# Two adds on VectorE in place of two identity products on TensorE, in the attention loop of a graph network

## The chip, the cores and the metric

The kernel runs on one core of one Trainium2 chip. The metric is the device time of one execution in microseconds (us), the median of several runs. The profile is of one execution; times in it are counted from the start of its span.

## The reference, cut to what matters

Two graph layers run over 3327 nodes with 512 features. Both use the same sparse adjacency matrix: about eight neighbours a node, itself included. Each layer ends with a residual and a normalisation.

```python
# layer 0, per head h (4 heads of 128 features)
feats  = einsum('nf,hfo->hno', X, W)
logits = leaky_relu(e_s[:, :, None] + e_n[:, None, :], 0.2)     # e_s, e_n: feats times a vector
attn   = softmax(logits where A, axis=-1)
out    = relu(einsum('hnm,hmo->hno', attn, feats) + b)
x      = layernorm(x + out)
# layer 1: a gated sum of an attention over the neighbours and of their plain sum
x      = layernorm(x + sigmoid(attn_a * x_a + attn_b * x_b))
```

The change concerns the line of `out`: the sum over a node's neighbours of attention weight times feature row, plus the bias `b`, before the relu.

## The kernel before, in words

**First part (to about 210 us).** The kernel finds every node's neighbours in the adjacency matrix, sorts the nodes by degree, and writes the features of all nodes to a table in device memory. The nodes are then worked on in 26 tiles of 128. Since they are sorted, all nodes of tile `j` fit into `CAPS[j]` neighbours besides the node itself: 4 to 14. Nodes with more are in tiles 0 and 12 (`T0`), the first of the two groups of 12 and 14 tiles, which carry one more gathered "stair" row.

**Layer 0 (about 216 to 560 us).** The loop at L878 goes through the tiles in `order0`: tiles 11 and 10, then 0 to 9, then the second group with long and short tiles in turn. Each engine takes its instructions in the order in which the loop issues them; nothing reorders them. Step `i` of the loop does the following.

- `gather` (L667, L661) for the tile of step `i + 3`: POOL issues an indirect DMA for each neighbour slot, which brings one feature row for each of the 128 nodes. For the second group the first two slots come in one DMA (L661): the node's input row and its own feature row. The rows land in buffers of up to six slots, of which there are seven (`GB`); a tile takes one to three. A gather into a used buffer waits until its last reader is done.
- `publish`: the normalised rows of earlier tiles are written to the table of layer 1 (ScalarE L847, VectorE L850 and L851, then a DMA: from SP for the first group, a scatter from POOL, L145, for the second).
- `columns2` of step `i - 2`: ScalarE copies transposed rows (L836), TensorE multiplies them by eight columns (L839).
- `attend` of step `i`: the weighted sum. TensorE first puts the bias into the accumulator by a product of the identity with it (L804). Then, slot by slot, the gathered row is multiplied in place by its four weights, one for each head: by VectorE in one instruction (L812), or for each third slot by ScalarE in four (L810). TensorE adds each row to the accumulator by a product with the identity (L815). The accumulator is in PSUM, and there are two.
- VectorE reads the accumulator of step `i - 1`, applies the relu and adds the input row (L893). For the second group that input row lies in the tile's first gather buffer. The statistics (L712, L713) follow, and after every few tiles the inverse square root (L721 to L728). TensorE transposes the result (L832), and VectorE copies the columns of step `i - 2` (L843).
- In steps 1 to 7 the lists of the second group are sorted with TensorE (L548); in step 7 VectorE copies the sorted lists (L553, L554). In step 8 it spreads the stair of the second group (`climb`, L599 and L600).
- `weigh_a` and `weigh_b` of step `i + 1`: the softmax weights from the gathered rows of that tile (VectorE L769 to L795, ScalarE's exponential L782). They need all of the tile's gathers to have landed.

**Layer 1 (from about 560 us)** gathers from the second table and has its own loop (L1072). In it VectorE also sums rows in pairs in place (L1022).

Of the kernel before, what the change touches and what calls it, by code (L numbers as in the profile page):

```python
# [25 lines left out]
CAPS = (14, 12, 11, 10, 9, 9, 8, 8, 7, 6, 6, 5) + (14, 13, 11, 10, 10, 9, 9, 8, 8, 7, 7, 6, 5, 4)  # L26
# [53 lines left out]
def sparse_pass(  # L80
# [39 lines left out]
    nc = tc.nc  # L120
    N, F = out.shape
# [8 lines left out]
    T0 = (0, NG[0])  # L130
# [27 lines left out]
    ident = const.tile([P, P], F32, name="ident")  # L158
    ones = const.tile([P, P], F32, name="ones")
    bias0 = const.tile([P, F], F32, name="bias0")  # L160
# [22 lines left out]
    def row1(j):  # L183
        g, i = place(j)
        return x1[g][:, i, :]
# [162 lines left out]
    for b, n in enumerate(STAIRS):  # L348
        o = sum(STAIRS[:b])
# [244 lines left out]
    def climb(g, pool, psum):  # L594

        of = pool.tile([P, B + H], F32, tag="of", name=f"of{g}")
        nc.vector.tensor_copy(of[:, :B], srt[g][:, 0, C0 + 1 : S + 1])
        nc.vector.tensor_copy(of[:, B:], srt[g][:, 0, S + 2 : S + 2 + H].bitcast(F32))
        nc.tensor.matmul(psum, to_row, of, start=True, stop=True)  # L599
        nc.vector.tensor_mul(of[:, :B], psum[:, :B], step_of)  # L600
        id_ = pool.tile([P, 1], F32, tag="id_", name=f"id_{g}")
        nc.vector.tensor_reduce(id_, of[:, :B], AX.X, ALU.add)
        nc.vector.tensor_copy(ids2[g], id_)
        nc.vector.tensor_copy(es2[g], psum[:, B:])
# [39 lines left out]
    def gather(table, j):  # L644


        g, i = place(j)
        ahead = 0 if table is table1 else 1 + g
        c = CAPS[j] + ahead
        more = j in T0  # L650
        n = (c + more + U - 1) // U
        w = (c + more + n - 1) // n
        got = []
        for q0 in range(0, c + more, w):
            m = min(w, c - q0)
            buf = gp.tile([P, U, ROW], F32, tag="g", name=f"g_{nc.next_id()}", bufs=GB)
            for q in range(q0, q0 + m):
                s = q - ahead + 1
                if ahead == 2 and q < 2:
                    if q == 0:  # L660
                        nc.gpsimd.indirect_dma_start(  # L661
                            out=buf[:, 0:2, :].rearrange("p t w -> p (t w)"), out_offset=None,
                            in_=own1.rearrange("n t w -> n (t w)"),
                            in_offset=bass.IndirectOffsetOnAxis(ap=srt[g][:, i, S + 1 : S + 2], axis=0),
                        )
                    continue
                nc.gpsimd.indirect_dma_start(  # L667
                    out=buf[:, q - q0, :], out_offset=None, in_=table[:, :],
                    in_offset=bass.IndirectOffsetOnAxis(ap=srt[g][:, i, s : s + 1], axis=0),
                )  # L670
            o = 1 if ahead == 2 and q0 == 0 else 0
            if m > o:
                got.append((q0 + o - ahead + 1, m - o, buf, o))
        if more:
            stair[j] = buf[:, m, :]
            nc.gpsimd.indirect_dma_start(
                out=stair[j], out_offset=None, in_=table[:, :],
                in_offset=bass.IndirectOffsetOnAxis(ap=ids2[g][:, 0:1], axis=0),
            )
        return got  # L680
# [73 lines left out]
    order0 = first[-2:][::-1] + first[:-2] + second[-3:-2]  # L754
# [42 lines left out]
            small = psx.tile([P, B * H], F32, tag="pcol", name=f"to_rows{j}", bufs=2)  # L797
            ws2[j] = to_rows(m0, small, f"n{j}", w[:, C0 + 1 :, :])

    def attend(j):  # L800

        w = ws[j]
        acc = accs[j] = ps.tile([P, F], F32, tag="acc", name=f"acc{j}", bufs=2)
        nc.tensor.matmul(acc, ident, bias0, start=True, stop=False)  # L804
        for s0, n, buf, o in got[j]:
            for s in range(s0, s0 + n):
                gv = buf[:, o + s - s0, 0:F].rearrange("p (h o) -> p h o", h=H)
                if s % 3 == 2:
                    for h in range(H):
                        nc.scalar.activation(gv[:, h, :], gv[:, h, :], AF.Copy, scale=w[:, s, h : h + 1])  # L810
                else:
                    nc.vector.tensor_tensor(  # L812
                        gv, gv, w[:, s, :].rearrange("p (h o) -> p h o", o=1).to_broadcast([P, H, FO]), ALU.mult
                    )
                nc.tensor.matmul(  # L815
                    acc, ident, buf[:, o + s - s0, 0:F], start=False, stop=(s == CAPS[j] and j not in T0)
                )
        if j in T0:
            gv = stair[j][:, 0:F].rearrange("p (h o) -> p h o", h=H)
            nc.vector.tensor_tensor(  # L820
                gv, gv, ws2[j].rearrange("p (h o) -> p h o", o=1).to_broadcast([P, H, FO]), ALU.mult
            )
            nc.tensor.matmul(acc, to_node, stair[j][:, 0:F], start=False, stop=True)
# [5 lines left out]
    def columns1(j):  # L829
        pt = turned[j] = psx.tile([P, KT, P], F32, tag="pt", name=f"x1t{j}", bufs=2)  # L830
        for k in range(KT):
            nc.tensor.transpose(pt[:, k, :], row1(j)[:, k * P : (k + 1) * P], ident)  # L832

    def columns2(j):
        xt1 = m0.tile([P, KT, P], F32, tag="xt1", name=f"xt1_{j}")
        nc.scalar.copy(xt1, turned[j])  # L836
        pcol = psx.tile([P, B * H], F32, tag="pcol", name=f"pcol{j}", bufs=2)[:, :NCOL]
        for k in range(KT):
            nc.tensor.matmul(pcol, xt1[:, k, :], v1[:, k, :], start=(k == 0), stop=(k == KT - 1))  # L839
        turned[j] = pcol  # L840

    def columns3(j):
        nc.vector.tensor_copy(row1(j)[:, F : F + NCOL], turned[j])  # L843

    def publish(j, scale, shift):
        row = row1(j)[:, 0:F]
        nc.scalar.activation(row, row, AF.Identity, scale=scale, bias=shift)  # L847
        col = row1(j)[:, F : F + NCOL]
        t = m0.tile([P, NCOL], F32, tag="shifted", name=f"shifted{j}")
        nc.vector.scalar_tensor_tensor(t, v1sum, shift, bias8, ALU.mult, ALU.add)  # L850
        nc.vector.scalar_tensor_tensor(col, col, scale, t, ALU.mult, ALU.add)  # L851
        if j < NG[0]:
            put = nc.sync.dma_start(table1[j * P : (j + 1) * P, :], row1(j)).ins
            tc.add_to_no_dep_group("table1", put)
        else:
            scatter("table1", table1[:, :], own(j), row1(j), N - 1)
# [21 lines left out]
    for i in range(NT + 3):  # L878
        if i + AHEAD < NT:
            j = order0[i + AHEAD]  # L880
            got[j] = gather(table0, j)
        for args in ready[0]:
            publish(*args)
        ready = [ready[1], []]
        if 2 <= i < NT + 2:
            columns2(order0[i - 2])
        if i < NT:
            attend(order0[i])
        if 0 < i <= NT:
            j = order0[i - 1]  # L890
            y = row1(j)[:, 0:F]
            xj = y if j < NG[0] else got[j][0][2][:, 0, 0:F]
            nc.vector.scalar_tensor_tensor(y, accs[j], 0.0, xj, ALU.max, ALU.add)  # L893
            columns1(j)
            done = norm.add(i - 1, y)
            if done:
                k0, scale, shift = done
                ready[1] = [
                    (order0[k], scale[:, k - k0 : k - k0 + 1], shift[:, k - k0 : k - k0 + 1]) for k in range(k0, i)
                ]  # L900
        if 2 <= i < NT + 2:
            columns3(order0[i - 2])
        if 0 < i <= 7:
            sort1(rankis[1], 2 * i - 2, 2 * i)
        if i == 8:
            climb(1, m0, psx.tile([P, B * H], F32, tag="pcol", name="climb1", bufs=2)[:, : B + H])
        if i == NG[0]:
            nc.vector.memset(over, 0.0)
            for j, c in enumerate(CAPS):
                if j in T0:  # L910
                    nc.vector.tensor_scalar(over[:, j, c:S], no_step, 0.0, None, ALU.is_lt)
                else:
                    nc.vector.memset(over[:, j, c:S], 1.0)
        if i + 1 < NT:
            weigh_a(order0[i + 1])
            weigh_b(order0[i + 1])
# [155 lines left out]
    for i in range(NT + 3):  # L1072
        j, j1, jp, jpp = at_(i), at_(i + 1), at_(i - 1), at_(i - 2)
# [496 lines left out]
```

## Time and profile before

| | before |
|---|---|
| median of three runs (lowest to highest) | 967.37 us (966.75 to 968.58) |
| the profiled execution | 968.11 us |
| its span, first to last instruction | 966.1 us |
| TensorE busy (share of the span) | 807.6 us (84%) |
| VectorE busy | 726.6 us (75%) |
| POOL busy | 610.8 us (63%) |
| ScalarE busy | 278.9 us (29%) |
| mean granted TensorE clock | 0.910 |

The table's busy times are means over stages with different limits. A row of a view names source line, engine, operation, output<-input and shape. In a timeline the square bracket holds the idle time before the instruction and what ended it. In the groups, "x95 | 65.7, 691 | 3.3" is 95 instructions, 65.7 us busy, 691 ns each and 3.3 us of idle time ahead of them. TensorE is PE, VectorE is DVE, ScalarE is ACT, GpSimd is POOL. `acc` is the accumulator, `g` a gather buffer, `x1a` and `x1b` the rows of layer 1 for the two groups, `x1t` the transposes, `pcol` the eight columns, `sorted` the sort.

### The profile page before, as it was taken

Reading aid. Unit: us, or ns where it says so; the run is one execution under the profiler, and the core shown is the slowest. Engines: PE = TensorE matmul, PEld = TensorE weight load, DVE = VectorE, ACT = ScalarE, POOL = GpSimd, SP = SyncE. Lnnn points to the kernel's source line nnn. Section 1 sums busy time; section 2 is a strip of 40 time slices with the busy share of each in tenths; the row PEclk is TensorE's granted clock in tenths of the full one; section 3 lists DMA queues with packets and bytes.
Section 4 is the critical chain, followed back from the end, with each engine's and each line's share of the span. In section 5 each row is a group of like instructions: output and inputs, shape, how many; then the busy total and the mean of one; then the engine's idle time right before and its main releaser. Section 6 shows DMA issues by size and latency. Waiting matters only on the chain.

```text
span 966.1 us, 10166 instructions
## 1 busy us (share of the span) xinstructions
PE 807.6 (84%) x2562; PEld 424.7 (44%) x2562; DVE 726.6 (75%) x2152; ACT 278.9 (29%) x820; POOL 610.8 (63%) x654
## 2 busy tenths in 40 slices
PE   4399896338999888989988938998999989899893
PEld 3177674114454444444434414444444444344341
DVE  4277869786878486668646747799999989989873
ACT  1022221003434342525334412222223232132241
POOL 6611134776677757677777467777777777777511
PEclk9799988557999999989998957999999999999997
DMA  8799999999678767787777347777666676666401
GB/s 323 286 350 374 393 332 364 381 396 296 172 210 251 208 199 219 247 294 227 234 219 221 129 145 191 198 196 189 195 191 199 187 193 193 188 185 182 142 20 49
DMA packets 71986, 221.41 MB, mean 229 GB/s; under 512 B 12912, under 2 KB 16960, under 8 KB 71024
## 3 DMA queue, kind: packets, MB, share of 16 engines
q0 software_dynamic: 46560, 153.64, 54.1%
q1 hardware_dynamic: 22704, 64.94, 17.8%
q10 hardware_dynamic: 2656, 2.10, 0.7%
q8 instruction: 23, 0.38, 0.2%
q14 instruction: 43, 0.35, 0.1%
HBM read 199.78 MB, written 28.32 MB: 236 GB/s over the span
## 4 chain that ended last, share of the span: by engine, by line
PE 38%; issue 20%; POOL 16%; DVE 11%; DMA 10%; ACT 3%; POOLq 0%; DVEq 0%; ACTq 0%
PE acc L815 21%; POOL g L667 10%; DMA g<-table,srt 8%; DVE sw L1020 5%; PE po L1060 5%; PE acc L1041 4%; PE pcol L839 3%; PE acc L804 3%; DVE g L1022 2%; DMA table<-row 1%; POOL table L379 1%; ACT xt L836 1%; PE x1t L832 1%; DMA a_row<-in_a_self 1%; POOL sprod L339 1%
## 5 line engine op out<-in xcount | busy, mean ns | idle before, releaser
L667 POOL DMA_INDIRECT g<-table,srt x464 | 478.8, 1032 | 165.3 <-issue 123.0
L815 PE MATMUL acc<-g,ident 128*128 128x512 f32 x504 | 230.8, 614 | 1.6 <-DVE g L812 1.6
L1020 DVE SCALAR_TENSOR_TENSOR sw<-g,e,sw 128x512 f32<-128x512 f32 x226 | 169.5, 750 | 13.1 <-ACT sw L1004 8.9
L815 PEld LDWEIGHTS acc<-g,ident 128*128 128x128 f32 x504 | 100.1, 199 | 131.9 <-issue 99.4
L1041 PE MATMUL acc<-g,ident 128*128 128x512 f32 x262 | 127.8, 615 | 23.8 <-DVE g L1022 14.2
L369 PE MATMUL pf<-w,xc 128*128 128x260 f32 x416 | 102.0, 407 | 13.2 <-DVE w L309 13.2
L812 DVE TENSOR_TENSOR g<-g,w 128x512 f32<-128x512 f32 x176 | 110.4, 695 | 0.6
L369 PEld LDWEIGHTS pf<-w,xc 128*128 128x128 f32 x416 | 83.5, 203 | 29.1 <-DVE w L309 14.0
L1060 PE MATMUL po<-wg,sT 128*128 128x512 f32 x208 | 95.5, 602 | 0.0
L1060 PE MATMUL po<-wsa,sT 128*128 128x512 f32 x208 | 94.3, 596 | 0.3 <-ACT sT L1053 0.3
L810 ACT ACTIVATE g<-g,w 128x128 f32<-128x128 f32 x304 | 91.6, 389 | 0.7 <-DVE w L795 0.7
L1041 PEld LDWEIGHTS acc<-g,ident 128*128 128x128 f32 x262 | 49.4, 194 | 94.8 <-issue 44.2
L1022 DVE TENSOR_TENSOR g<-g 128x512 f32<-128x512 f32 x95 | 65.7, 691 | 3.3
L379 POOL DMA_DIRECT2D table<-row x26 | 14.4, 554 | 84.7 <-ACT st L378 84.7
L1090 ACT ACTIVATE za<-za 128x512 f32<-128x512 f32 x26 | 16.4, 631 | 166.4 <-DVE za L1088 166.4
L1060 PEld LDWEIGHTS po<-wg,sT 128*128 128x128 f32 x208 | 40.3, 195 | 50.7 <-issue 50.2
L1060 PEld LDWEIGHTS po<-wsa,sT 128*128 128x128 f32 x208 | 39.9, 192 | 50.8 <-issue 48.1
L145 POOL DMA_INDIRECT out<-za,srt x26 | 27.9, 1075 | 50.0 <-ACT za L1105 43.9
L397 PE MATMUL pc<-at,pow 128*32 128x512 bf16 (+1 forms) x182 | 24.7, 438 | 34.7 <-DMA at<-in_adjB 20.7
L839 PE MATMUL pcol<-v,xt 128*128 128x8 f32 x208 | 30.4, 273 | 25.5 <-ACT xt L836 25.4
L836 ACT COPY xt<-x1t 128x512 f32<-128x512 f32 x26 | 15.2, 584 | 97.3 <-PE x1t L832 97.3
L839 PEld LDWEIGHTS pcol<-v,xt 128*128 128x128 f32 x208 | 29.0, 213 | 32.0 <-ACT xt L836 30.9
(251 smaller groups left out, 944.9 us busy)
## 6 DMA issues: line engine op xcount, KB each, us to landing
at<-in_adjB SPq DMA_DIRECT2D x78, 512.0 KB, 11.2
g<-table,srt POOLq DMA_INDIRECT x464, 3.8
table<-row POOLq DMA_DIRECT2D x26, 260.0 KB, 5.8
xc<-in_xB SPq DMA_DIRECT2D x6, 1024.0 KB, 7.5
own<-in_xo SPq DMA_DIRECT2D x1, 3640.0 KB, 32.4
own<-table SPq DMA_DIRECT2D x1, 3640.0 KB, 47.6
at<-in_adjL SPq DMA_DIRECT2D x13, 256.0 KB, 13.1
table<-x1a SPq DMA_DIRECT2D x12, 260.0 KB, 4.4
```

The lines of the kernel that those rows point to most:

```text
L145: put = nc.gpsimd.indirect_dma_start(out=dst, out_offset=bass.IndirectOffsetOnAxis(ap=rows, axis=0), in_=src, in_offset=None, bounds_check ...
L369: nc.tensor.matmul(pf[:, hh, :HC], xc[:, k, o : o + P], w0[:, k, hh, :], start=(k == 0), stop=(k == KT - 1))
L667: nc.gpsimd.indirect_dma_start(out=buf[:, q - q0, :], out_offset=None, in_=table[:, :], in_offset=bass.IndirectOffsetOnAxis(ap=srt[g][:, i ...
L804: nc.tensor.matmul(acc, ident, bias0, start=True, stop=False)
L810: nc.scalar.activation(gv[:, h, :], gv[:, h, :], AF.Copy, scale=w[:, s, h : h + 1])
L812: nc.vector.tensor_tensor(gv, gv, w[:, s, :].rearrange("p (h o) -> p h o", o=1).to_broadcast([P, H, FO]), ALU.mult)
L815: nc.tensor.matmul(acc, ident, buf[:, o + s - s0, 0:F], start=False, stop=(s == CAPS[j] and j not in T0))
L839: nc.tensor.matmul(pcol, xt1[:, k, :], v1[:, k, :], start=(k == 0), stop=(k == KT - 1))
L1020: nc.vector.scalar_tensor_tensor(sw, g[:, i, 0:F], e[:, s : s + 1], sw, ALU.mult, ALU.add)
L1022: nc.vector.tensor_add(g[:, i, 0:F], g[:, i - 1, 0:F], g[:, i, 0:F])
L1041: nc.tensor.matmul(plain[j], to, row, start=(not sums_of_two and i == 0), stop=(sums_of_two and i == len(rows) - 1),)
L1060: nc.tensor.matmul(proj[j], sT[:, k, :], wt[:, k, :], start=(half + k == 0), stop=(half + k == KT))
```

## The change

From the fourth tile of the loop on (`lean`, steps 3 to 25) the bias product is left out. VectorE adds the bias to the weighted row of slot 0 in place; it then adds that row to the weighted row of slot 1. TensorE starts the accumulator with this sum and goes on with slot 2. The result is the same sum. Slots 0 and 1 are always weighted by VectorE. The first three tiles are computed as before.

```diff
-    def attend(j):
+    def attend(j, lean):
         w = ws[j]
         acc = accs[j] = ps.tile([P, F], F32, tag="acc", name=f"acc{j}", bufs=2)
-        nc.tensor.matmul(acc, ident, bias0, start=True, stop=False)
+        if not lean:
+            nc.tensor.matmul(acc, ident, bias0, start=True, stop=False)
...
+                row = buf[:, o + s - s0, 0:F]
+                if lean and s == 0:
+                    nc.vector.tensor_add(row, row, bias0)
+                    row0 = row
+                    continue
+                if lean and s == 1:
+                    nc.vector.tensor_add(row, row, row0)
                 nc.tensor.matmul(
-                    acc, ident, buf[:, o + s - s0, 0:F], start=False, stop=(s == CAPS[j] and j not in T0)
+                    acc, ident, row, start=(lean and s == 1), stop=(s == CAPS[j] and j not in T0)
                 )
...
-            attend(order0[i])
+            attend(order0[i], i >= 3)
```

## The prediction

> **What bounds the kernel now.** I read the page's busy shares first, then the chain that ended last, then the layer-0 loop in stretches, and last the timelines of POOL and VectorE there. Only layer 0 matters: the edit is in its loop, and layer 1 starts when that loop has written its table. I number the tiles by their place in the loop, 1 to 26.
>
> The bias product alone (view of its source line; min/median/max ns), and the nearest row to the added operation, an in-place 128x512 add on VectorE in layer 1:
>
> ```profile
> L804 PE MATMUL acc<-bias,ident x52: 592/676/1202, 216.0 to 548.2; 128*128 128x512 f32 x52
> L1022 DVE TENSOR_TENSOR g<-g 128x512 f32<-128x512 f32 x95 | 65.7, 691 | 3.3
> ```
>
> 52 records are 26 products: each f32 product leaves two. The chain shows what one really costs (start, us, what):
>
> ```profile
> 260.89 0.96 PE acc L804 x2
> 261.85 11.16 PE acc L815 x26
> 273.01 0.44 PE x1t L832 x4
> 273.45 1.41 PE sorted L548 x4
> 274.86 0.79 PE pcol L839 x8
> ```
>
> 13 row products take 11.16 us, 0.858 each; the bias product costs 0.96, and 1.91 where TensorE comes out of idleness (at 418.78). One whole tile, and every piece is TensorE's. But it isn't so everywhere. Busy us of PE, weight load, DVE, ACT, POOL, then clock, DMA share and GB/s:
>
> ```profile
> 260.00:300.00 40.00, 40.00 (x121) 19.90 (x120) 30.65 (x90) 17.59 (x57) 30.55 (x32) 1.00 0.79 227
> 440.00:480.00 40.00, 37.81 (x114) 18.49 (x113) 29.06 (x75) 16.65 (x54) 30.55 (x32) 1.00 0.79 229
> 480.00:520.00 40.00, 33.15 (x97) 16.98 (x96) 21.65 (x70) 16.58 (x52) 30.58 (x31) 0.91 0.76 222
> ```
>
> TensorE is full only in the first. POOL's 30.5 of 40 us is also full: each gather is 0.95 busy plus a fixed 0.30 before the next, 1.257 us, whatever else happens. Layer 0 has 254 gathers and 14 scatters, four of them between gathers: 258 x 1.257 = 324 us of the 354 from 180 to 534. So POOL's queue is the second bound, right behind TensorE. What it still loses (idle before, releaser), and the VectorE lines that matter:
>
> ```profile
> 352.52 0.95 POOL L667 DMA_INDIRECT g<-table,srt  x1 [7.32 <-ACT x1a L847]
> 395.19 0.95 POOL L667 DMA_INDIRECT g<-table,srt  x1 [4.25 <-PE acc L815]
> 423.99 0.95 POOL L667 DMA_INDIRECT g<-table,srt  x1 [1.24 <-DMA g<-table,srt]
> 532.78 0.95 POOL L667 DMA_INDIRECT g<-table,srt  x1 [0.30 <-issue]
> ```
>
> ```profile
> 326.21 0.54 DVE L553 CAST srt<-sorted 128x364 int32<-128x364 f32 x1 [9.71 <-PE sorted L548]
> 394.24 0.68 DVE L893 SCALAR_TENSOR_TENSOR x1b<-acc,g 128x512 f32<-128x512 f32 x1
> 423.05 0.68 DVE L893 SCALAR_TENSOR_TENSOR x1b<-acc,g 128x512 f32<-128x512 f32 x1
> 553.11 0.69 DVE L893 SCALAR_TENSOR_TENSOR x1b<-acc,g 128x512 f32<-128x512 f32 x1 [3.20 <-PE acc L815]
> ```
>
> Those gathers wait for one of seven buffers. The named releasers mislead: 395.19 and 423.99 are each 0.27 us after an L893 ended (394.92, 423.73), which reads the first buffer of the 13th and 15th tile. The one at 352.52 overwrites the first buffer of the 10th tile, whose fifth product ends about then.
>
> [...] layer-0 gathers average 0.98 us, those of layer 1, with its adds, 1.08.
>
> **The change, part by part.** For 23 tiles (4 to 26):
> - Removed: bias product and one row product, 0.96 + 0.858 = 1.82 us of TensorE, 41.8 in all.
> - Added: two adds on VectorE, each waiting for the multiplication before it. A dependent 512-wide instruction starts 0.03 after the end of the last (L893 to its statistics: 0.71), an independent one 0.62 after the last's start. Multiply, add, multiply, add then the next is 0.71+0.62+0.71+0.62 = 2.66, against 1.24 now: +1.42 us a tile, 32.7 in all. Bounds: 1.24 (all overlapped) to 1.5.
> - Moved: TensorE's first product of a tile needs row 1 summed, 2.8 us after VectorE begins the tile (2.04 + 0.69 + a signal), where the bias product needed nothing and row 0 0.75. L893 of the tile before and the next tile's weights queue behind the two adds, 1.42 later; L893 is what POOL waits for. No DMA is added or moved, and POOL's waits are the same list.
>
> Now tile by tile, with each engine's own order.
>
> *Tiles 4 to 8, TensorE full.* Rows begin at 260.89, where the bias was. 12 products (10.30) end at 271.2; 2.64 between tiles; then 11, 10, 9, 9 products: ends at 283.3, 294.5, 304.9, 315.2. Before: 324.16. Gain 9.0 = 5 x 1.8. VectorE must be ready: it began the 8th tile at 306.32 because L893 and the copy L843 waited for TensorE each turn; with earlier products and +1.42 I get 303.6, first sum at 306.4, TensorE asks at 307.5. It fits by 1.1.
>
> *Handover.* L553 waits for the last sort product, queued behind tile 8's rows: 326.21 becomes 317.25, and tile 9 starts on VectorE at 319.85 (before 328.80). Its first product at 322.65, 8 products as cold as now (9.42 - 0.86): 331.2, before 340.33. A second such wait (L600) passes the 9.1 on: VectorE starts tile 10 at 334.6.
>
> *POOL.* Tile 10's first product at 337.4, half clock, fourth at about 342. A 1.40 stall at 337.65 goes, so the gather of 352.52 is due at 343.8 and finds its buffer: the stall is gone, POOL is 8.75 ahead. From here POOL sets the pace. L893 of tile 13 ends at 386.3, so 395.19 becomes 386.5 (8.7 ahead). L893 of tile 15 comes at 415.75, because VectorE started tile 16 only 8.7 early and has 1.42 more in it: 423.99 becomes 416.7, 7.3 ahead; a 0.47 stall at 434.70 goes: 7.8. No later L893 is late: at tile 19 it ends at 462.9, wanted at 481.7. The last gather: 532.78 becomes 525.0.
>
> *The end.* Tile 25's weights wait for its gathers: VectorE starts it at 533.59 - 7.8 = 525.8, and 5.64 later does L893 of tile 24, 531.45 (537.81). Tile 26 starts at 542.37 - 6.4 = 536.0; L893 of tile 25 at 539.85; its statistics and square root (4.28 before) end at 544.1. TensorE has tile 26 by 538.8 + 4 x 0.858 = 542.25. So L893 of tile 26 is at 544.1 instead of 553.11: 9.0. The chain after it, to the first layer-1 gather at 564.68, is untouched.
>
> *Allowance.* The 215 gathers from 230 to 535 exceed the usual 0.95 by 0.03 on average, 6.5 us in sum, beside 244 wide VectorE instructions in layer 0; 46 more, +19%, is 1.2 us.
>
> Sum: 9.0 - 1.2 = 7.8 us. The profiled execution took 968.11 (span 966.1 and 2.0 around it), 0.74 above the median of the runs: 960.3 there, **959.6** against the median of 967.37. 41.8 us leave TensorE and about a fifth reaches the end; the rest becomes waiting for gathers.
>
> **Rivals.**
> - *POOL keeps no stall at all.* If L893 is never late[...], all that POOL still loses after tile 4 comes back: 7.02 + 3.95 + 0.94 + 1.40 + 0.47 = 13.8, plus the 1.2 by which the end gains more than POOL: 15.0, 952.4. For it: gathers are then the only thing left. Against: two of the stalls hang on L893. It is the floor.
> - *Half clock and late sums eat half.* With TensorE waiting several us a tile, more tiles start at half clock; the 10th tile's fourth product has 1.3 us of slack before POOL stalls again, and two slow tiles at the end cost 2 each. Gain 3: 964.4.
> - *VectorE becomes the bound (slower).* If its tile grows as long as POOL's (254 / 26 x 1.257 = 12.3 us), each of the 13 tiles from the 14th pays 1.42, 18.5, against 8.75 won before: +9.7, 977. It decides once L893 comes after the gather that wants its buffer at every tile. Against: VectorE is busy 21 to 31 of 40 us, and its waits for landing gathers from tile 20 on are 1.4 to 6.3 us a tile, what the 1.42 can fall into.
> - *Nothing arrives.* If the 9.0 stays as slack before tile 10's buffer, within 0.2% (about what a measurement of this kernel can tell from no change): 967.
>
> **Numbers.** Main case 0.62, its own range 956.5 to 962 (add 1.24 to 1.5[...]). No stall 0.12, half eaten 0.12, nothing 0.05, VectorE bound 0.09. Faster 0.86, same 0.05, slower 0.09. The range 954.5 to 965 holds the main case and most of its two neighbours.
>
> **What would show it.** Right: 229 instead of 252 row products and 3 instead of 26 bias products; the sort copy L553 near 317; no wait near 344 on POOL; the last layer-0 gather near 525; the first layer-1 gather near 556; TensorE idler from 340 on, waiting for VectorE. Wrong: POOL idle at more gathers after 390 with L893 ending just before each, adds well over 0.7 us, or a layer 1 that isn't 401 us long.

## The result, and the profile after

| | before | after |
|---|---|---|
| median of six runs each (lowest to highest) | 967.98 us (965.94 to 974.92) | 960.01 us (958.35 to 961.49) |
| the profiled execution | 968.11 us | 959.54 us |
| its span | 966.1 us | 957.5 us |
| TensorE busy | 807.6 us | 779.3 us |
| VectorE busy | 726.6 us | 757.4 us |
| mean granted TensorE clock | 0.910 | 0.894 |

The ratio after to before is 0.9917 (95% interval 0.9892 to 0.9942): 8.0 us less, 5.6 to 10.5. The forecast was 959.6. The experiments below were run in four batches; in all but the third the chip ran every kernel, the one before included, at about 1100 us, so each ratio is read only against the kernel before of the same batch.

In the changed kernel the lines behind L815 have moved: the row product is L824 (L815 before), the bias product L806, the multiplication L814, the bias add L819, the row add L823, the transposes L841, the eight columns L848, and what was L847, L850 and L893 is L856, L859 and L902.

The groups of the changed kernel (busy us and mean ns of one; then the idle time ahead of them and what ended it):

```profile
L824 PE MATMUL acc<-g,ident 128*128 128x512 f32 x458 | 224.8, 649 | 10.6 <-DVE g L823 9.0 <-DVE g L814 1.6
L819 DVE TENSOR_TENSOR g<-g,bias 128x512 f32<-128x512 f32 x23 | 16.0, 697 | 0.8
L823 DVE TENSOR_TENSOR g<-g 128x512 f32<-128x512 f32 x23 | 15.9, 692 | 0.8
```

458 records are 229 products. The adds cost what the nearest row promised, 0.69 us each, 31.9 us in all, and VectorE's busy time has risen by 30.8. TensorE's has fallen by 28.3, less than the 41.8 of the products, for more of the remaining ones run at half clock (649 ns a record on average, 614 before; 46 of the 458 records take 1 us or more, 20 of 504 before). The 9.0 us ahead of the row products are new: TensorE waits seven times for a sum.

The stretches of the changed kernel (busy us of PE, weight load, DVE, ACT, POOL; clock, DMA share, GB/s):

```profile
260.00:300.00 40.00, 40.00 (x123) 20.19 (x122) 37.28 (x104) 19.52 (x62) 30.65 (x31) 1.00 0.80 232
440.00:480.00 40.00, 34.51 (x100) 17.08 (x99) 30.57 (x87) 15.68 (x49) 30.55 (x32) 0.91 0.79 228
480.00:520.00 40.00, 29.59 (x83) 15.15 (x82) 27.73 (x69) 16.50 (x52) 30.55 (x32) 0.83 0.75 227
```

In the first stretch TensorE is still full, and VectorE, 30.65 us busy before, is now nearly full too. In the two others TensorE has lost about 3.4 us of work and POOL is as busy as it was.

The timeline of POOL, the gathers that answer to the four shown of before (start, us, what; in the bracket the idle time before it):

```profile
343.64 0.95 POOL L667 DMA_INDIRECT g<-table,srt  x1 [1.04 <-ACT x1a L856]
...
387.29 0.95 POOL L667 DMA_INDIRECT g<-table,srt  x1 [4.25 <-DVE x1b L902]
...
417.78 0.95 POOL L667 DMA_INDIRECT g<-table,srt  x1 [2.45 <-DVE x1b L902]
...
525.96 0.95 POOL L667 DMA_INDIRECT g<-table,srt  x1 [0.30 <-issue]
```

and that of VectorE:

```profile
315.19 0.54 DVE L553 CAST srt<-sorted 128x364 int32<-128x364 f32 x1 [4.52 <-PE sorted L548]
...
386.34 0.68 DVE L902 SCALAR_TENSOR_TENSOR x1b<-acc,g 128x512 f32<-128x512 f32 x1
...
416.83 0.68 DVE L902 SCALAR_TENSOR_TENSOR x1b<-acc,g 128x512 f32<-128x512 f32 x1
...
545.25 0.69 DVE L902 SCALAR_TENSOR_TENSOR x1b<-acc,g 128x512 f32<-128x512 f32 x1
```

The stall of 7.32 us at 352.52 has shrunk to 1.04 (0.30 of it is the pace of the queue). The stall of 4.25 is as it was, and the one of 1.24 has grown to 2.45: both gathers still start 0.27 us after an L902. The first layer-1 gather comes at 556.81 (564.68 before), and layer 1 takes 400.7 us (401.4).

**A lead that no edit made.** The changed kernel is ahead before its first changed tile. TensorE's timeline in the first and around the third tile, in the kernel before and then in the changed one:

```profile
219.69 8.09 PE L815 MATMUL acc<-g,ident 128*128 128x512 f32 x12 [1.59 <-DVE g L812]
...
239.59 1.85 PE L839 MATMUL pcol<-v,xt 128*128 128x8 f32 x8
241.29 2.06 PE L804 MATMUL acc<-bias,ident 128*128 128x512 f32 x2
...
260.75 1.10 PE L804 MATMUL acc<-bias,ident 128*128 128x512 f32 x2
```

```profile
219.76 6.91 PE L824 MATMUL acc<-g,ident 128*128 128x512 f32 x12 [1.59 <-DVE g L814]
...
239.28 1.49 PE L806 MATMUL acc<-bias,ident 128*128 128x512 f32 x2
240.57 14.39 PE L824 MATMUL acc<-g,ident 128*128 128x512 f32 x30
...
258.31 4.11 PE L824 MATMUL acc<-g,ident 128*128 128x512 f32 x9
```

The code of these three tiles is the same in both. In the execution of before, the first tile's six row products took 1.2 us longer, and the third tile's eight columns and bias product ran at half clock (granted clock 0.50 from 239 to 245; 1.85 and 2.06 us; 1.06 and 1.10 in two later profiles of kernels with the same three tiles). At the start of the fourth tile the changed kernel is 2.44 us ahead. So this pair of profiles overstates what the change did in the loop; from here on I count from TensorE's first product of tile 4 (260.75 before, 258.31 after). From there to the first layer-1 gather it is 303.93 us before and 298.50 after, 5.4 less.

### The profile page after: what moved, and what is told of

Its sections match the earlier page's. It is cut to its first block, busy times and chain, and to the rows that moved or that the text cites. A ratio compares the mean times of both kernels' runs of the same rounds, so it can differ in the third digit from the quotient of the medians.

```text
span 957.5 us, 10005 instructions
## 1 busy us (share of the span) xinstructions
PE 779.3 (81%) x2470; PEld 412.7 (43%) x2470; DVE 757.4 (79%) x2198; ACT 279.1 (29%) x820; POOL 612.6 (64%) x654
## 4 chain that ended last, share of the span: by engine, by line
PE 24%; POOL 23%; DVE 22%; DMA 14%; issue 13%; ACT 2%; DVEq 0%; POOLq 0%; ACTq 0%
POOL g L667 17%; DMA g<-table,srt 10%; PE acc L824 10%; PE pf L369 7%; DVE sw L1029 7%; DVE g L814 3%; PE po L1069 3%; PE acc L1050 2%; DVE g L1031 2%; DMA at<-in_adjB 2%; DMA a_row<-in_a_self 1%; DMA table<-row 1%; POOL sprod L339 1%; POOL lists L145 1%; DVE za L1097 1%
## 5 line engine op out<-in xcount | busy, mean ns | idle before, releaser
L824 PE MATMUL acc<-g,ident 128*128 128x512 f32 x458 | 224.8, 649 | 10.6 <-DVE g L823 9.0
L824 PEld LDWEIGHTS acc<-g,ident 128*128 128x128 f32 x458 | 93.7, 209 | 124.6 <-issue 81.4
L1050 PE MATMUL acc<-g,ident 128*128 128x512 f32 x262 | 127.3, 613 | 23.9 <-DVE g L1031 14.1
L369 PE MATMUL pf<-w,xc 128*128 128x260 f32 x416 | 104.9, 415 | 13.3 <-DVE w L309 13.3
L814 DVE TENSOR_TENSOR g<-g,w 128x512 f32<-128x512 f32 x176 | 113.5, 693 | 0.6
L369 PEld LDWEIGHTS pf<-w,xc 128*128 128x128 f32 x416 | 85.5, 208 | 30.2 <-DVE w L309 14.1
L1050 PEld LDWEIGHTS acc<-g,ident 128*128 128x128 f32 x262 | 49.2, 193 | 94.5 <-issue 41.4
L848 PE MATMUL pcol<-v,xt 128*128 128x8 f32 x208 | 30.9, 275 | 32.9 <-ACT xt L845 32.9
L782 ACT ACTIVATE w<-w 128x40 f32<-128x40 f32 (+10 forms) x26 | 6.2, 238 | 160.9 <-DVE w L781 160.9
L848 PEld LDWEIGHTS pcol<-v,xt 128*128 128x128 f32 x208 | 29.4, 216 | 39.3 <-ACT xt L845 38.3
```

Source lines behind the costliest of these rows:

```text
L369: nc.tensor.matmul(pf[:, hh, :HC], xc[:, k, o : o + P], w0[:, k, hh, :], start=(k == 0), stop=(k == KT - 1))
L814: nc.vector.tensor_tensor(gv, gv, w[:, s, :].rearrange("p (h o) -> p h o", o=1).to_broadcast([P, H, FO]), ALU.mult)
L824: nc.tensor.matmul(acc, ident, row, start=(lean and s == 1), stop=(s == CAPS[j] and j not in T0))
L1050: nc.tensor.matmul(plain[j], to, row, start=(not sums_of_two and i == 0), stop=(sums_of_two and i == len(rows) - 1),)
```

## The experiments

My theory was that TensorE bounds only tiles 4 to 8, that the whole gain is made there and carried on because POOL's stall behind them disappears, and that the other 18 tiles pay for their adds and gain nothing. The rival: each tile gains its share.

### Where the gain is made

The adds in tiles 4 to 8 alone:

```diff
-            attend(order0[i], i >= 3)
+            attend(order0[i], 3 <= i < 8)
```

> Only tiles 4 to 8 use the adds; from tile 9 on the loop is that of the kernel before. My theory (TensorE is the bound only in tiles 4 to 8; behind them POOL's queue): the whole gain is made here. The gather that stalled at 352.52 us comes near 344, and without the adds L902 of tile 15 is 1.4 us earlier than in the changed kernel, so the last layer-0 gather lies near 524 and the time at 959, the same as the changed kernel or about 1 us less. Rival (the gain is spread over the 23 tiles as the removed products are): 5 of 23 tiles, 8.0 x 5/23 = 1.7 us, a time of 966.

> Tiles 4 to 8 with the adds, all others as before; a second time, since in the first call every kernel, the one before too, took about 1099 us. My theory: 0.991 of the kernel before (959 where it takes 967.5), no longer than the changed kernel; the stall of 7 us near 352 is gone, the last layer-0 gather comes near 524. Rival (gain spread over all 23 tiles): 0.998.

> Tiles 4 to 8 with the adds, all others as before; a third time, because in the first two calls VectorE stood still up to 20 us at a time without a wait, in every kernel. If the stretch is undisturbed, my theory is as written: 0.991 of the kernel before, the gather after the former stall of 7 us near 344 and the last layer-0 gather near 524. Rival (the gain is spread over 23 tiles): 0.998.

And in tiles 9 to 26 alone:

```diff
-            attend(order0[i], i >= 3)
+            attend(order0[i], i >= 8)
```

> Only tiles 9 to 26 use the adds; tiles 4 to 8 are as before. My theory: no gain, 967 to 969.5. 18 x 1.82 = 32.8 us leave TensorE, but POOL's stall of 7 us near 352 stays, the sum of each tile comes 1.4 us later on VectorE, and the last statistics take the place of TensorE at the end. Rival (spread): 18 of 23 tiles, 6.3 us, 961.7.

> Tiles 9 to 26 with the adds, tiles 4 to 8 as before; a second time for the same reason. My theory: 1.000 to 1.002 of the kernel before (967 to 969.5); POOL still stalls some 7 us near 352. Rival (spread): 0.9935, 961.7.

> Tiles 9 to 26 with the adds, tiles 4 to 8 as before; a third time for the same reason. My theory: 1.000 to 1.002 of the kernel before, with a stall of POOL of some 7 us near 352. Rival (spread): 0.9935.

| adds in | median | before, same batch | ratio (95%) |
|---|---|---|---|
| tiles 4 to 8, first batch | 1093.9 | 1099.2 | 0.9930 (0.9858 to 1.0001) |
| tiles 4 to 8, second batch | 1094.1 | 1097.2 | 0.9990 (0.9938 to 1.0041) |
| **tiles 4 to 8, third batch** | **958.37** | **966.94** | **0.9922 (0.9898 to 0.9946)** |
| tiles 9 to 26, first batch | 1098.6 | 1099.2 | 0.9992 (0.9920 to 1.0064) |
| tiles 9 to 26, second batch | 1094.4 | 1097.2 | 0.9961 (0.9927 to 0.9995) |
| **tiles 9 to 26, third batch** | **967.04** | **966.94** | **1.0000 (0.9983 to 1.0018)** |

The first two batches can't answer the question, because the queue of gathers that the theory speaks of doesn't set the pace there: beyond its 0.30 us a gather, POOL stands idle in layer 0 for 100 to 106 us in these four profiles, against 23 in the kernel before and 12 in the third batch with adds in tiles 4 to 8. VectorE's timeline in the second batch, adds in tiles 4 to 8:

```profile
346.63 0.17 DVE L852 COPY x1a<-pcol 128x8 f32<-128x8 f32 x1 [19.83 <-remote]
```

It stood still for 19.83 us with nothing recorded that it waited for; each of these four profiles has several such places, none of them in the profiles of the kernel before and of the third batch's two kernels. What causes them the trace doesn't show.

In the third batch the two halves come apart as the theory has it: five tiles bring the whole gain (0.9922 against 0.9917 for all 23), eighteen bring nothing. The rival's 0.998 and 0.9935 both lie outside the intervals.

The chain of waits of both kernels shows what a tile of TensorE loses (start, us, what). Adds in tiles 4 to 8:

```profile
259.43 10.40 PE acc L824 x24
269.83 0.44 PE x1t L841 x4
270.27 1.41 PE sorted L548 x4
271.68 0.79 PE pcol L848 x8
272.47 9.54 PE acc L824 x22
```

Adds in tiles 9 to 26, where tile 4 is still that of the kernel before:

```profile
261.92 0.96 PE acc L806 x2
262.88 11.16 PE acc L824 x26
274.04 0.44 PE x1t L841 x4
```

10.40 us in place of 0.96 + 11.16 = 12.12: 1.72 a tile. From the first product of tile 4 to the transposes of tile 8 it is 63.41 us without the adds (before, and this kernel) and 54.83 with them (after, and the other kernel): 8.58 in both comparisons, and TensorE waits for no sum in these tiles. That is ten products at 0.858. The bias product costs no more than a row product: the 0.10 that it seemed to cost more is there without it too (12 row products, 10.40 us), and falls there on the row product that comes first.

POOL's timeline, adds in tiles 4 to 8:

```profile
344.41 0.95 POOL L667 DMA_INDIRECT g<-table,srt  x1 [0.30 <-issue]
...
386.98 0.95 POOL L667 DMA_INDIRECT g<-table,srt  x1 [4.25 <-DVE x1b L902]
...
393.93 0.95 POOL L667 DMA_INDIRECT g<-table,srt  x1 [0.75 <-issue]
...
523.14 0.95 POOL L667 DMA_INDIRECT g<-table,srt  x1 [0.31 <-DMA g<-own,srt]
```

and in tiles 9 to 26:

```profile
354.89 0.95 POOL L667 DMA_INDIRECT g<-table,srt  x1 [8.49 <-ACT x1a L856]
...
429.02 0.95 POOL L667 DMA_INDIRECT g<-table,srt  x1 [3.05 <-DVE x1b L902]
...
537.57 0.95 POOL L667 DMA_INDIRECT g<-table,srt  x1 [0.30 <-issue]
```

The first kernel has no stall behind tile 8 and none near 418. The second has the old stall, 1.2 us longer, and a longer one at 429. Both fit what the expectation named. Counted from the start of tile 4, in us:

| | to the last layer-0 gather | from it to the first layer-1 gather |
|---|---|---|
| before | 272.03 | 31.90 |
| adds in tiles 4 to 8 | 263.86 (-8.2) | 31.06 |
| adds in tiles 9 to 26 | 275.79 (+3.8) | 30.11 |
| after | 267.65 (-4.4) | 30.85 |

At the last gather the halves add up to the whole: -8.2 + 3.8 = -4.4. In these profiles the 18 later tiles lose 3.8 us of POOL's time. The 3.8 between the changed kernel and the one with five tiles can be named: the rest of the stall at 343.64, 0.74; the stall at 417.78, 2.15; minus a wait of 0.45 at 393.93 that only the five-tile kernel has; and 1.35 in the gathers themselves.

From the start of tile 4 to the last layer-0 gather, the gathers exceed the usual 0.95 us by 6.2 us in sum before, 7.3 with 10 adds, 7.1 with 36, and 8.7 with all 46. It is most with all the adds, but there is no fixed price for one. What does go with the adds is the number of gathers of 1.01 to 1.04 us: 2, 4, 21 and 27; 18 or 19 are longer than that in every profile.

In time the loss of 3.8 us isn't resolved. The medians give 0 (-1.6 to +1.7) for the 18 tiles alone, and the five tiles and all 23 have overlapping intervals. The profiles are one execution each; that of the 18 tiles ran 6 us above its own median, some 2.5 of it ahead of the loop and 2 in layer 1, so up to 1.5 of its 3.8 may be this one execution's.

### What the adds cost by themselves

The changed kernel without its adds; bias and slot 0 are left out of the sum in 23 tiles:

```diff
                 if lean and s == 0:
-                    nc.vector.tensor_add(row, row, bias0)
-                    row0 = row
                     continue
-                if lean and s == 1:
-                    nc.vector.tensor_add(row, row, row0)
```

> The changed kernel without its 46 adds: bias and slot 0 are left out of the sum in 23 tiles, TensorE does what it does in the changed kernel. What the adds cost, by itself. My theory: they cost about 5 us: L902 of tiles 13 and 15 comes 1.4 us earlier each, the last two tiles 2 x 1.4 us, and POOL's gathers lose some 2 us less to the adds beside them; 955, 953 to 957. Rival A (the adds are hidden behind the wait for gathers): 960. Rival B (VectorE paces the second half, 18.5 to 32.7 us): 930 to 942.

> The changed kernel without its 46 adds (bias and slot 0 left out of the sum in 23 tiles); a second time for the same reason. My theory: the adds cost about 5 us, 0.987 of the kernel before (955, 953 to 957). Rival A (hidden behind the gathers): 0.992, 960. Rival B (VectorE paces the second half): 0.975 or less.

> The changed kernel without its 46 adds (bias and slot 0 left out of the sum in 23 tiles), in an undisturbed stretch. From the profile of the kernel with the adds in tiles 4 to 8 alone, whose last layer-0 gather is at 523.1 against 526.0, I expect the adds to cost 3 to 5 us: 0.987 of the kernel before (955), last layer-0 gather near 522. Rival A (all 46 adds hidden behind the gathers): 0.992. Rival B (VectorE paces the second half): 0.975 or less.

And the adds without the saving; slot 0 is counted twice in 23 tiles:

```diff
-        if not lean:
-            nc.tensor.matmul(acc, ident, bias0, start=True, stop=False)
+        nc.tensor.matmul(acc, ident, bias0, start=True, stop=False)
...
                     row0 = row
-                    continue
...
-                    acc, ident, row, start=(lean and s == 1), stop=(s == CAPS[j] and j not in T0)
+                    acc, ident, row, start=False, stop=(s == CAPS[j] and j not in T0)
```

> The kernel before with the 46 adds put in and no product taken out (slot 0 is counted twice in 23 tiles). The same price from the other side. My theory: tiles 4 to 8 hide them, since VectorE is busy 20 to 31 of 40 us under a full TensorE; after that 1.4 us at each of the two late L902, 1 to 2 us at the end and 2 us in the gathers: 970 to 973 against 968 before. Rival A (hidden): 968. Rival B (VectorE paces): 986 to 1000.

> The kernel before with the 46 adds put in and no product taken out (slot 0 counted twice in 23 tiles), in an undisturbed stretch. My theory: 3 to 5 us, 1.003 to 1.005 of the kernel before (970 to 972): nothing in tiles 4 to 8, 1.4 us at each of the two late L902, 2 us in the gathers, 1 at the end. Rival A (hidden): 1.000. Rival B (VectorE paces): 1.02 to 1.03.

| | ratio to before (95%), batch by batch |
|---|---|
| products out, no adds (first, second, fourth batch) | 0.9901 (0.9846 to 0.9957), 0.9863 (0.9779 to 0.9946), 0.9831 (0.9742 to 0.9920) |
| adds in, no product out (first and fourth batch) | 1.0054 (0.9998 to 1.0111), 1.0162 (1.0076 to 1.0247) |

All five ran at about 1100 us, so the numbers expected of an undisturbed chip were not tested. Of their own condition they say this: taking the 46 products out is worth 11 to 19 us there, and putting the 46 adds in costs 6 to 18. The adds are then neither hidden nor paid in full, and little would be left of the trade, which agrees with the small gains of the two part changes there; the changed kernel itself was not run in these batches. What the adds cost on an undisturbed chip rests on the profiles of the section above alone.

### Adds where TensorE was thought to bound

```diff
-            attend(order0[i], i >= 3)
+            attend(order0[i], 2 <= i < 8 or i >= 24)
```

> The adds only where TensorE is thought to bound: tiles 3 to 8 and the last two, 25 and 26. My theory: tile 3, with 15 rows and a stair product between 243 and 258 us, is TensorE's too, so 1.8 us more than with tiles 4 to 8 alone, less what POOL's queue (0.95 + 0.30 us a gather) no longer lets through; the last two bring nothing, as the last statistics on VectorE take over there: 0.990, 957 to 959.5. Rival (POOL's queue already bounds after tiles 4 to 8): the same as with tiles 4 to 8 alone.

It ran in the second batch: 1094.1 us, 0.9989 (0.9957 to 1.0021), as the kernel with tiles 4 to 8 in that batch (0.9990). Whether the third tile brings anything on an undisturbed chip stays open.

## Why the prediction was right, step by step

**The mechanism held.** The gain is made in tiles 4 to 8 and carried through the handover; POOL's large stall goes; from tile 9 on TensorE's saving turns into waiting and into products at half clock. The products counted (229 and 3) are those named. The forecast of 7.8 us for the median met 8.0. How far that was luck is said under "What compensated".

**Removed work.** Predicted 1.82 a tile and 9.0 for five tiles; 1.72 and 8.58. The step that took 0.96 from a chain piece counted the 0.10 that the first product costs more as the bias product's own.

**Added work.** VectorE's timeline in tile 25 of the changed kernel:

```profile
526.77 0.69 DVE L814 TENSOR_TENSOR g<-g,w 128x512 f32<-128x512 f32 x1
527.49 0.69 DVE L819 TENSOR_TENSOR g<-g,bias 128x512 f32<-128x512 f32 x1
528.10 0.68 DVE L814 TENSOR_TENSOR g<-g,w 128x512 f32<-128x512 f32 x1
528.82 0.69 DVE L823 TENSOR_TENSOR g<-g 128x512 f32<-128x512 f32 x1
529.43 3.10 DVE L814 TENSOR_TENSOR g<-g,w 128x512 f32<-128x512 f32 x5
```

From 526.77 to 529.43 it is 2.66 us, the 0.71 + 0.62 + 0.71 + 0.62 of the sum. "It fits by 1.1" for tile 8 held as well: TensorE goes from the columns to the rows there without a wait.

**Handover.** L553 was predicted at 317.25 and came at 315.19. Without the lead of 2.44 it is 317.63, 0.38 late, about the 0.42 missing from the five tiles.

**POOL's stall at tile 10** was predicted gone, with the gather at 343.8 and 1.3 us of slack. It came at 343.64, but only because of the lead: without it that is 346.08, 2.3 late. Of these, 0.74 are stall that was left; 1.2 are slower gathers since tile 4; and 0.30 is a slip in my sum, which took away the whole 7.32 of the bracket though 0.30 of it is the queue's pace. The stall is left because of TensorE. Its timeline of tile 10, changed kernel:

```profile
333.49 1.06 PE L848 MATMUL pcol<-v,xt 128*128 128x8 f32 x8 [2.88 <-ACT xt L845]
336.19 9.28 PE L824 MATMUL acc<-g,ident 128*128 128x512 f32 x14 [1.65 <-DVE g L823]
```

and with tile 10 as before (adds in tiles 4 to 8):

```profile
333.75 1.88 PE L848 MATMUL pcol<-v,xt 128*128 128x8 f32 x8 [2.88 <-ACT xt L845]
335.47 2.06 PE L806 MATMUL acc<-bias,ident 128*128 128x512 f32 x2
337.32 9.03 PE L824 MATMUL acc<-g,ident 128*128 128x512 f32 x17
```

With the adds TensorE stands idle for 1.65 us more and takes its first row products at half clock (granted clock 0.50 from 335.5 to 342.3). The buffer comes free with the fourth: its second record ends at 342.89, and the gather starts at 343.64, 0.75 later. The product of the same slot ends 0.75 before the gather in the kernel before too (351.77 and 352.52), and with adds in tiles 9 to 26 (354.14 and 354.89). That is 6.7 us after the first product began, where I had allowed 4.6. What differs from the kernel with tile 10 as before is what falls into the slow stretch. There the columns and the bias product take 1.88 and 2.06 us (1.06 and 1.11 in its next tile, from 347.94), and the nine rows, from 337.32 to the transposes at 346.61, take 1.6 us more than nine times 0.858: the columns, the bias product and about two rows are slow, and the buffer is free in time for a gather at 344.41 that doesn't wait. With the adds the eight rows, from 336.19 to the transposes at 346.17, take 3.1 us more than eight times 0.858, so more than three are slow, and so it is with adds in tiles 9 to 26 (2.9 us more, from 347.68 to 357.41). I had counted the bias product as pure work; its 2.06 us also take up slow time while VectorE multiplies. Where the stretch begins and how long it is varies from one execution to the next (in the profile of before the granted clock is 0.50 for 3.4 us in this tile, from 344.6 to 348.0), so the share of the missing product in it isn't separated. This is the rival "half clock and late sums", in a small size.

**The two L902.** Predicted ends 386.3 and, for the tile-15 gather, 416.7; measured 387.02 and 417.78. With the lead taken off they are 3.2 and 3.5 later than forecast. The first is the 0.74 and the 0.30 of tile 10, and gathers that had by then become 2.2 us slower in sum. I had 1.2 for the whole loop, booked only at its end; it was 2.5. My "whatever else happens" for the pace of a gather was too strong. From tile 19 on no L902 was late, as said, and no stall follows 417.78.

**The end.** Every step lies 1.0 us after its forecast (L902 of tile 24 at 532.44 for 531.45, tile 26 at 537.00 for 536.0, L902 of tile 26 at 545.25 for 544.1), because the last gather does (525.96 for 525.0); with the lead taken off the delay is 3.4, of which the 1.2 booked at the end allowed for a third. That the statistics of tile 25 take over from TensorE as the last wait was right. The gain of 1.2 over POOL is not shown: the two profiles without adds at the end have 31.90 and 31.06 from the last layer-0 gather to the first of layer 1, the two with them 30.85 and 30.11, and each two of the same code differ by almost as much as the two kinds do.

**What compensated.** The 8.6 us between the two spans are 2.4 of lead, 0.7 of a shorter layer 1 and 5.4 from tile 4 on, where the sum forecast 7.8: in this pair the loop falls 2.4 short of the forecast, and a lead of 2.4 that no edit made covers it. That is luck. The medians don't hang on one pair and give 8.0, with an interval of 5.6 to 10.5. So the sum is confirmed as a size, and not to the microsecond: the terms that I had too small, the half clock at tile 10 and the slower gathers, are there in the profiles. Why the medians gain more than the 5.4 of this pair stays open. For adds in tiles 4 to 8 alone the two agree better: 9.0 from tile 4 on in the profiles (303.93 before, 294.92), 8.6 in the medians.

**Rivals.** "POOL keeps no stall" fell: two L902 stalls stay. "VectorE becomes the bound" fell on an undisturbed chip: 18 tiles with adds cost 0 (-1.6 to +1.7), where it needed 18.5. "Nothing arrives" fell.

## What to carry to other kernels

When work moves from one engine to another, count the gain only in the stretch where the relieved engine is full, and then ask for the next queue: 10 of the 46 products removed here made the whole gain. Restrict such an edit to that stretch; the kernel with five tiles is as fast as that with 23 (0.9922 and 0.9917, not told apart) and spares VectorE 36 adds. And look at where the two executions stand before the first changed instruction, ahead of comparing their ends.

## What the runs showed of the hardware

- In tile 10 the granted clock was 0.50 from 344.6 to 348.0 before and from 335.5 to 342.3 after, and the bias product took up slow time that otherwise fell on the rows: it took 2.06 us there (before; adds in tiles 4 to 8), against 1.10 at the start of tile 4. With it ahead of them the rows took 0.7 and 1.6 us more than 0.858 each, or one to two row products at twice their time; without it 3.1 and 2.9 more, or more than three (after; adds in tiles 9 to 26). The mean granted clock of the profiled execution was 0.910 before and 0.914 with adds in five tiles, 0.894 and 0.898 in the two kernels with adds from tile 9 on.
- With VectorE's 128x512 adds in the loop, gathers of 1.01 to 1.04 us in place of 0.95 became frequent: 2 with no add, 4 with 10, 21 with 36, 27 with 46. Of the 27, 19 overlap an add in time; of the 146 gathers below 0.97 us in the same profile, 6 do.
